# Expert blocks of two batches spread over two attention stages, and the sorting's counts copied out of their bank

## The chip, the cores and the metric

The kernel runs on one core of a Trainium2 chip. Its engines work side by side, each through its own queue in order: TensorE (PE, with weight loads PEld), VectorE (DVE), ScalarE (ACT), GpSimd (POOL) and SyncE (SP), which here issues most transfers. The metric is the time of one execution on the device in microseconds, the median over several runs; lower is better.

## What is computed

Four sequences of 1024 tokens with 128 features pass two layers. Each layer normalises, scales and shifts by a modulation of its batch's condition, and adds a gated result, first of a mixer and then of a mixture of experts. In the first layer the mixer is causal attention with 16 query heads, 4 key heads and rotary embedding; the experts are the best two of eight for every token.

```python
# layer 0
h = layernorm(x) * (1 + ca) + sa
x = x + ga * attention(h, Wq, Wk, Wv, Wo)
h = layernorm(x) * (1 + cb) + sb
scores = softmax(h @ gate_w.T)
topk_w, topk_idx = top_k(scores, 2);  topk_w /= sum(topk_w)
for e in range(8):
    g, u = split(h @ w1[e])
    out += combine[:, e] * (silu(g) * u @ w2[e])
x = x + gb * out
# layer 1: a selective scan in place of attention, then experts with a capacity
```

All arithmetic is in float32.

## The kernel before

**Attention** runs in eight stages, numbered 0 to 7 by `at`: for each of four batches b two head groups c (L686). A stage works eight tiles of 128 queries in the order 7, 0, 6, 1, 5, 2, 4, 3 (L685). A tile has four steps g. In each, `probabilities` (L586) multiplies queries by keys, masks and takes the smallest with VectorE, exponentiates with ScalarE and scales by the reciprocal sum on GpSimd (L618). One tile later `second_half` (L649) transposes the probabilities (L627), multiplies them by the values into the bank `po`, copies this to `aT` (L643) and projects it into `pw`, which is added to x (L189 and L190). Other work is woven between as Python generators that advance a step at a time: the next stage's projection, zeroing of buffers in HBM, and the two below.

**The first layer's experts.** Once both head groups of a batch are done, `sort_tokens` (L325) runs in the next stage with c = 0 (stages 2, 4 and 6 for batches 0, 1 and 2; batch 3 is sorted in the scan part). It normalises the batch, takes router logits, chooses two experts per token and counts, with matmuls by a triangle and by ones, how many tokens of each expert come before each token (bank `pin`). From `pin[:, TB, :]`, the totals, `find_blocks` works out which blocks of 128 slots belong to which expert; from `pin[:, :TB, :]` each token's slot follows. Sixteen indirect transfers then scatter the rows into HBM (L379). In the stage after it (3, 5 and 7) the class `Blocks` works the 23 blocks: `turn` transposes three blocks' rows, `first` multiplies one block by its expert's first weights and applies silu, `second` by the second weights and the gate. The weights come from HBM with three buffers (`fw`, L262), by transfers whose expert number SP reads from a register. `first` and `second` of a block share one PSUM bank. `first_returns` gathers the results back (L281) and adds them to x, by the program in the second head group's stage of the batch two later (stages 5 and 7).

**PSUM.** Pool `ps_m` has one bank, tag `m`. In attention the value projection, the features, the sorting's transposes, logits and counts, the blocks' `turn` and `first`/`second`, and `pw` take it by turns.

**Order.** The program's order gives priorities only. The tile framework places instructions on each engine's queue ahead of time: the earliest in the program that is ready by its own reckoning goes first, and a tile whose buffer is taken waits for its release. Work whose inputs are there early can thus run far ahead of its place in the program. On the chip each queue keeps the order so found.

**The loop before** steps the blocks so (L721 to L729), three blocks for every tile, and makes the object at the end of the preceding stage (L751 to L753):

```python
if blocks is not None:
    if g == 0:
        blocks.turn(n)
    else:
        blocks.second(3 * n + g - 1)
probabilities(i, g, q, k, pr)
if blocks is not None and g < 3:
    blocks.first(3 * n + g)
```

Of the kernel before, what the change touches and what calls it, by code (L numbers as in the profile page):

```python
# [11 lines left out]
F32 = mybir.dt.float32  # L12
# [6 lines left out]
P = 128  # L19
# [7 lines left out]
NE = 8  # L27
# [17 lines left out]
def mm(nc, out, lhsT, rhs, start=True, stop=True):  # L45
    return nc.tensor.matmul(out, lhsT, rhs, start=start, stop=stop)  # L46
# [3 lines left out]
def adaln_two_layers(ctx: ExitStack, tc: tile.TileContext, I: dict, out: bass.AP):  # L50
# [14 lines left out]
    def load(pool, name, eng=nc.sync):  # L65
# [6 lines left out]
    make_identity(nc, ident)  # L72
    ones = cst.tile([P, P], F32, name="ones")
    nc.gpsimd.memset(ones, 1.0)

    causal = cst.tile([P, P], F32, name="causal")
    nc.gpsimd.memset(causal, 0.0)
    nc.gpsimd.affine_select(
        out=causal, in_=causal, compare_op=ALU.is_ge, fill=NEG, base=0, pattern=[[-1, P]], channel_multiplier=1
    )  # L80

    before = cst.tile([P, P], F32, name="before")
    nc.gpsimd.affine_select(
# [44 lines left out]
    def drained(steps):  # L128

        while True:  # L130
            try:
                next(steps)
            except StopIteration as end:
                return end.value
# [174 lines left out]
    def find_blocks(total, nb, pool):  # L309


        over = pool.tile([P, NE, TB], F32, tag="f_over", bufs=1, name="f_over")
        nc.vector.tensor_tensor(over, total.unsqueeze(2).to_broadcast([P, NE, TB]), after, ALU.is_gt)
        blocks = pool.tile([P, NE], F32, tag="f_blocks", bufs=1, name="f_blocks")
        nc.vector.tensor_reduce(blocks, over, AX.X, ALU.add)
        upto = pool.tile([P, NE], F32, tag="f_upto", bufs=1, name="f_upto")
        nc.vector.tensor_tensor_scan(upto, ones[:, :NE], blocks, 0.0, ALU.mult, ALU.add)
        yield
        past = pool.tile([P, NB, NE], F32, tag="f_past", bufs=1, name="f_past")[:, :nb]
        nc.vector.tensor_tensor(past, number[:, :nb], upto.unsqueeze(1).to_broadcast([P, nb, NE]), ALU.is_ge)  # L320
        which = pool.tile([P, NB], F32, tag="f_which", bufs=1, name="f_which")[:, :nb]
        nc.vector.tensor_reduce(which, past, AX.X, ALU.add)
        return blocks, upto, which

    def sort_tokens(b, kept, pool, ps, tag, xtag="fxn"):  # L325


        xn = pool.tile([P, TB, D], F32, tag=xtag, bufs=1, name="fxn")
        yield from norm_steps(b * TB, TB, xn)
        hT = pool.tile([P, S], F32, tag=tag, bufs=1, name="fhT")  # L330
        yield from feature_steps(xn, hT, ps, modT[0][:, 4, b : b + 1], modT[0][:, 3, b : b + 1])
        pl = ps.tile([P, TB, NE], F32, tag="m", name="fpl")
        for t in range(TB):
            mm(nc, pl[:, t, :], hT[:, t * P : (t + 1) * P], f_gate)
        yield
        m1, m2, oh1, oh2 = yield from top2_steps(pl, sm)

        both = sm.tile([P, TB, NE], F32, tag="f_both", bufs=1, name="f_both")
        nc.vector.tensor_add(both, oh1, oh2)
        flat = both.rearrange("p t e -> p (t e)")  # L340
        pin = ps.tile([P, TB + 1, NE], F32, tag="m", name="fpin")
        pinf = pin.rearrange("p t e -> p (t e)")
        mm(nc, pinf[:, : TB * NE], before, flat, stop=False)
        for n in range(1, TB):
            mm(nc, pinf[:, n * NE : TB * NE], ones, flat[:, : (TB - n) * NE], start=False, stop=(n == TB - 1))
        mine = sm.tile([P, NE], F32, tag="f_mine", bufs=1, name="f_mine")
        nc.vector.tensor_reduce(mine, both.rearrange("p t e -> p e t"), AX.X, ALU.add)
        mm(nc, pin[:, TB, :], ones, mine)
        yield
        z = sm.tile([P, TB], F32, tag="f_z", bufs=1, name="f_z")  # L350
        nc.vector.scalar_tensor_tensor(z, m1, 1e-20, m2, ALU.add, ALU.add)
        nc.vector.reciprocal(z, z)
        w = keep.tile([P, 2, TB], F32, tag=f"f_w{b}", name="f_w")
        nc.vector.tensor_mul(w[:, 0], m1, z)
        nc.vector.tensor_mul(w[:, 1], m2, z)
        yield

        blocks, upto, which = yield from find_blocks(pin[:, TB, :], NB, sm)
        expert = keep.tile([P, NB], I32, tag=f"f_expert{b}", name="f_expert")
        nc.vector.tensor_scalar(expert, which, float(NE - 1), None, ALU.min)  # L360
        yield

        nc.vector.tensor_tensor(upto, upto, blocks, ALU.subtract)
        pos = sm.tile([P, TB, NE], F32, tag="f_pos", bufs=1, name="f_pos")
        nc.vector.scalar_tensor_tensor(
            pos, upto.unsqueeze(1).to_broadcast([P, TB, NE]), float(P), pin[:, :TB, :], ALU.mult, ALU.add
        )
        yield
        place = sm.tile([P, 2, TB], F32, tag="f_place", bufs=1, name="f_place")
        placei = keep.tile([P, 2, TB], I32, tag=f"f_placei{b}", name="f_placei")  # L370
        for k, oh in enumerate((oh1, oh2)):
            nc.vector.tensor_mul(oh, oh, pos)
            nc.vector.tensor_reduce(place[:, k], oh, AX.X, ALU.add)
            yield
        nc.vector.tensor_copy(placei, place)
        kept[b] = expert, placei, w
        for t in range(TB):
            for k in range(2):
                nc.gpsimd.indirect_dma_start(  # L379
                    out=f_in[b][:, :],  # L380
                    out_offset=bass.IndirectOffsetOnAxis(ap=placei[:, k, t : t + 1], axis=0),
                    in_=xn[:, t, :],
                    in_offset=None,
                )
                yield
# [71 lines left out]
    with ExitStack() as es:  # L457
# [21 lines left out]


        MW = 512 + QG
        mask = aw.tile([P, MW], F32, name="mask")
        nc.gpsimd.memset(mask, 0.0)
        for j in range(4):
# [200 lines left out]
        order = [7, 0, 6, 1, 5, 2, 4, 3]  # L685
        stages = [(b, c) for b in range(B) for c in range(2)]  # L686
        waiting = Steps(None, 0)
        blocks = None
        hT = features(0)
        made = []  # L690
        for _ in project(0, hT, made, at_once=True):
# [5 lines left out]
        for at, (b, c) in enumerate(stages):  # L697
            q, k = made
            if c == 0:
                v = values(hT)  # L700
            coming = Steps(None, 0)


            sorting = sort_tokens(b - 1, kept, ab, ps_m, "xn") if c == 0 and b > 0 else iter(())
            back = first_returns(b - 2, ab, 3) if c == 1 and b > 1 else iter(())
            early = first_features() if (b, c) == stages[-1] else iter(())
            for n, i in enumerate(order):
                if n == 5 and at + 1 < len(stages):

                    if c == 1:  # L710
                        hT = features(b + 1)
                    made = []
                    coming = Steps(project(stages[at + 1][1], hT, made), 5)
                long = i >= TB // 2
                keys = S if long else S // 2
                pr = [
                    ab.tile([P, 4, keys], F32, tag=f"pr{hp}{int(long)}", bufs=1, name=f"pr{hp}") for hp in range(2)
                ]
                for hp in range(2):
                    nc.gpsimd.memset(pr[hp][:, 0:3, i * P + QG : (i + 1) * P], 0.0)  # L720
                for g in range(4):  # L721
                    if blocks is not None:
                        if g == 0:
                            blocks.turn(n)
                        else:
                            blocks.second(3 * n + g - 1)
                    probabilities(i, g, q, k, pr)
                    if blocks is not None and g < 3:
                        blocks.first(3 * n + g)  # L729
                    waiting.take(-(-waiting.n // (4 - g)))  # L730
                    if n > 5 and g % 2 == 1 or n == 7 and g == 0:
                        coming.take(1)

                    if at < 2:
                        next(zeros, None)
                    if at == 0 and n == 0:
                        next(gates, None)

                    if n > 1:
                        next(sorting, None)  # L740
                        next(sorting, None)
                next(back, None)
                next(early, None)
                next(early, None)
                waiting = Steps(second_half(b, c, i, pr, v), i + 2)
            if at == 1:
                drained(zeros)
            drained(sorting)
            drained(back)
            drained(early)  # L750
            blocks = None  # L751
            if c == 0 and b > 0:
                blocks = Blocks(b - 1, ab, (ps_m, "m"), [(ps_m, "m")], rest)  # L753
        waiting.take(TB + 1)


# [718 lines left out]
```

## Time and profile before

| | us |
|---|---|
| median of 3 runs | 2087.29 |
| lowest and highest | 2079.24 and 2093.18 |
| the profiled execution | 2099.86 |
| its span, first to last instruction | 2098.1 |
| attention, to its last `aT` copy | 1390.7 |

The profile page gives each engine's busy time, then the span in 40 slices of 52.5 us with the busy share in tenths and the clock that was granted to TensorE. Below that stands what the groups of instructions cost and waited for. The two groups of GpSimd that matter here, with count, busy time and mean length, then idle time and its releaser:

```profile
L618 POOL TENSOR_SCALAR pr<-pr,den 128x32 f32<-128x32 f32 (+31 forms) x512 | 357.5, 714 | 311.0 <-DVE den L615 304.9
L379 POOL DMA_INDIRECT blocks_in<-fxn,f_placei x64 | 65.3, 1020 | 56.8 <-DMA blocks_in<-fxn,f_placei 46.5
```

### The profile page before, as it was taken

How to read it: one execution, taken by the hardware profiler on the slowest of the kernel's cores; microseconds unless marked ns; L12 is line 12 of the kernel's file. 1: busy time of each engine (PE TensorE's matmuls, PEld its weight loads, DVE VectorE, ACT ScalarE, POOL GpSimd, SP SyncE). 2: the span in 40 equal slices, each digit the busy share in tenths (PEclk: the TensorE clock that was granted, in tenths of full speed). 3: DMA queues.
4: the chain of work that ended last, by engine and by line, in shares of the span. 5: the costliest groups of instructions: out<-in, count | busy, mean ns of one | idle time of the engine just before them, and what ended most of it. 6: DMA issues, size and time to landing. Idle time of an engine off the chain costs nothing. (4 is left out here: it accounts for less than half of the span.)

```text
span 2098.1 us, 29043 instructions
## 1 busy us (share of the span) xinstructions
PE 1777.6 (85%) x8957; PEld 962.3 (46%) x8957; DVE 1325.2 (63%) x4000; ACT 948.5 (45%) x2073; POOL 1000.2 (48%) x1277
## 2 busy tenths in 40 slices
PE   5999899898999898999988899967769757748984
PEld 2444454453555344455534455533335423216764
DVE  6655666665667665666766466646768886972243
ACT  2353544743554554454365345544456345332221
POOL 3345434446333636532544643344663775672254
PEclk9899999999999998999999999988889977968996
DMA  7302001002222101222200122210012220003334
GB/s 232 133 1 51 1 5 47 1 29 73 60 70 75 41 1 46 79 63 70 77 13 24 43 75 67 61 40 3 29 48 86 79 103 17 4 25 95 115 127 149
DMA packets 103755, 123.58 MB, mean 59 GB/s; under 512 B 15024, under 2 KB 68656, under 8 KB 103600
## 3 DMA queue, kind: packets, MB, share of 16 engines
q1 hardware_dynamic: 83296, 97.70, 15.7%
q0 software_dynamic: 8192, 16.74, 2.6%
q10 hardware_dynamic: 12112, 7.29, 1.2%
q8 instruction: 71, 1.16, 0.2%
q14 instruction: 84, 0.69, 0.1%
HBM read 67.85 MB, written 32.90 MB: 48 GB/s over the span
## 5 line engine op out<-in xcount | busy, mean ns | idle before, releaser
L618 POOL TENSOR_SCALAR pr<-pr,den 128x32 f32<-128x32 f32 (+31 forms) x512 | 357.5, 714 | 311.0 <-DVE den L615 304.9
L612 ACT ACTIVATE pr<-pr,nb 128x32 f32<-128x32 f32 (+31 forms) x512 | 371.9, 728 | 156.1 <-DVE nb L599 147.7
L627 PE MATMUL pt<-ident,pr 128*128 128x128 f32 x2304 | 343.9, 284 | 52.4 <-POOL pr L618 43.2
L627 PEld LDWEIGHTS pt<-ident,pr 128*128 128x128 f32 x2304 | 255.0, 142 | 247.3 <-POOL pr L618 81.4
L46 PE MATMUL sc<-k,q 64*128 64x512 f32 (+14 forms) x1536 | 332.4, 524 | 31.5 <-DVE nb L599 24.3
L46 PE MATMUL po<-pT,v 128*64 128x512 f32 x1152 | 345.5, 626 | 2.6 <-DVE pT L631 2.6
L629 ACT COPY pT<-pt 128x512 f32<-128x512 f32 x288 | 167.7, 582 | 359.8 <-PE pt L627 306.0
L599 DVE CUSTOM_DVE_ANT_0 pr<-sc,mask 128x512 f32<-128x512 f32 (+15 forms) x512 | 273.0, 559 | 69.7 <-PE sc L46 58.4
L631 DVE COPY pT<-pt 128x512 f32<-128x512 f32 x288 | 198.3, 689 | 163.8 <-PE pt L627 147.4
L957 POOL TENSOR_TENSOR hc<-h,cc 128x512 f32<-128x512 f32 x128 | 162.0, 1279 | 101.0 <-DVE h L953 43.3
L46 PEld LDWEIGHTS sc<-k,q 64*128 64x128 f32 x1536 | 123.3, 192 | 183.3 <-DVE nb L599 87.3
L46 PE MATMUL pu<-du,spread 128*128 128x512 f32 x256 | 145.8, 672 | 52.2 <-DVE h L953 42.5
L720 POOL MEMSET pr<- 128x288 f32 x128 | 42.4, 340 | 258.4 <-PE pt L627 254.3
L599 DVE CUSTOM_DVE_ANT_0 pr<-sc,mask,nb 128x416 f32<-128x416 f32 (+15 forms) x256 | 120.0, 496 | 8.0 <-PE sc L46 6.9
L951 ACT ACTIVATE da<-dt,negA 128x512 f32<-128x512 f32 x128 | 91.6, 719 | 64.9 <-DVE h L953 64.4
L46 PEld LDWEIGHTS po<-pT,v 128*64 128x64 f32 x1152 | 69.5, 136 | 84.2 <-issue 42.9
L1343 POOL DMA_INDIRECT y<-slots_out,slot x56 | 56.7, 1013 | 94.0 <-PE ph L46 51.0
L949 DVE TENSOR_TENSOR pu<-pu,bb 128x512 f32<-128x512 f32 x128 | 85.1, 684 | 26.1 <-PE pu L46 15.7
L46 PEld LDWEIGHTS pu<-du,spread 128*128 128x128 f32 x256 | 44.9, 204 | 121.0 <-DVE h L953 73.7
L612 ACT ACTIVATION_READ_ACCUMULATOR pr<-pr,nb 128x1 f32 x512 | 96.5, 188 | 0.0
L568 POOL TENSOR_TENSOR q<-rot_u,rot_v 128x512 f32<-128x512 f32 x64 | 81.4, 1272 | 31.3 <-DMA rot_v<-rot_w 23.6
L379 POOL DMA_INDIRECT blocks_in<-fxn,f_placei x64 | 65.3, 1020 | 56.8 <-DMA blocks_in<-fxn,f_placei 46.5
(273 smaller groups left out, 2685.1 us busy)
## 6 DMA issues: line engine op xcount, KB each, us to landing
fw<-in_f_w SPq DMA_DIRECT2D x92, 320.0 KB
rot_v<-rot_w SPq DMA_DIRECT2D x300, 64.0 KB
gw<-in_g_w SPq DMA_DIRECT2D x15, 512.0 KB
fxe<-blocks_in SPq DMA_DIRECT2D x28, 192.0 KB
blocks_out<-fye SPq DMA_DIRECT2D x28, 192.0 KB
blocks_in<-mask SPq DMA_DIRECT2D x20, 256.0 KB
slots_in<-mask SPq DMA_DIRECT2D x16, 256.0 KB
g_w<-in_g_w SPq DMA_DIRECT2D x8, 512.0 KB
```

What stands on the lines that cost most here:

```text
L46: return nc.tensor.matmul(out, lhsT, rhs, start=start, stop=stop)
L379: nc.gpsimd.indirect_dma_start(out=f_in[b][:, :], out_offset=bass.IndirectOffsetOnAxis(ap=placei[:, k, t : t + 1], axis=0), in_=xn[:, t, : ...
L568: nc.gpsimd.tensor_add(to, u.rearrange("p (n q) -> p n q", q=QG), v.rearrange("p (n q) -> p n q", q=QG))
L599: nc.vector.tensor_tensor_reduce(out=pr[hp][:, g, lo:hi], in0=sc[:, hp, : hi - lo], in1=mask[:, MW - hi + lo :] if hi == nk else mask[:, : ...
L612: nc.scalar.activation(p, p, AF.Exp, bias=nb[:, last, hp : hp + 1], scale=-1.0, accum_out=den[:, hp : hp + 1])
L618: nc.gpsimd.tensor_scalar(p, p, den[:, hp : hp + 1], 1.0, ALU.mult, ALU.mult)
L627: next_to(hp == 0 and g == 0, lambda: nc.tensor.transpose(to, p, ident))
L629: nc.scalar.copy(pT[:, hp, :], pt)
L631: nc.vector.tensor_copy(pT[:, hp, :], pt)
L949: nc.vector.tensor_mul(pu, pu, bb[:, tok])
L951: nc.scalar.activation(da, dt[:, tok], AF.Exp, scale=negA[:, c : c + 1])
L957: nc.gpsimd.tensor_mul(hcs[-1], h, cc[:, tok])
```

## The change

Three things. First, the blocks of batches 0 and 1 are stepped over two stages each (3 and 4, 5 and 6) in place of one; batch 2 keeps stage 7 alone. A generator does the same steps in the same order and is advanced twice for every g; for batches 0 and 1 each step takes two advances, so that one step falls to each g, ahead of `probabilities`. A group of three blocks now takes two tiles of queries. The object, with its first weight loads, is made when the generator is first advanced. At the ends of stages 4, 6 and 7 what is left of it is run. Stages 4 and 6 thus hold sorting and blocks at once. Second, `sort_tokens` copies the whole count bank to a tile `ahead` in SBUF right after the counting, and later steps read the copy. Third, the causal mask's first form lives in a buffer of the tag `fam`, which the blocks use later, in place of one of its own, and is made after the first loads.

```diff
+        ahead = sm.tile([P, TB + 1, NE], F32, tag="f_ahead", bufs=1, name="f_ahead")
+        nc.vector.tensor_copy(ahead, pin)
...
-        blocks, upto, which = yield from find_blocks(pin[:, TB, :], NB, sm)
+        blocks, upto, which = yield from find_blocks(ahead[:, TB, :], NB, sm)
...
-            pos, upto.unsqueeze(1).to_broadcast([P, TB, NE]), float(P), pin[:, :TB, :], ALU.mult, ALU.add
+            pos, upto.unsqueeze(1).to_broadcast([P, TB, NE]), float(P), ahead[:, :TB, :], ALU.mult, ALU.add
...
-    causal = cst.tile([P, P], F32, name="causal")
+        causal = ab.tile([P, P], F32, tag="fam", name="causal")
...
-        blocks = None
+        def block_steps(b, fast):
+            blocks = Blocks(b, ab, (ps_m, "m"), [(ps_m, "m")], rest)
+            for j in range(0, NB, 3):
+                doing = [(blocks.turn, j // 3)]
+                for r in range(j, j + 3):
+                    doing += [(blocks.first, r), (blocks.second, r)]
+                for what, which in doing:
+                    what(which)
+                    yield
+                    if not fast:
+                        yield
+                yield
+                if not fast:
+                    yield
+
+        blocks = iter(())
...
-                    if blocks is not None:
-                        if g == 0:
-                            blocks.turn(n)
-                        else:
-                            blocks.second(3 * n + g - 1)
+                    next(blocks, None)
                     probabilities(i, g, q, k, pr)
-                    if blocks is not None and g < 3:
-                        blocks.first(3 * n + g)
+                    next(blocks, None)
...
-            blocks = None
+            if at + 1 == len(stages) or at == 4 or at == 6:
+                drained(blocks)
             if c == 0 and b > 0:
-                blocks = Blocks(b - 1, ab, (ps_m, "m"), [(ps_m, "m")], rest)
+                blocks = block_steps(b - 1, b == B - 1)
```

More of the change, by code (lines that the diff above doesn't have):

```diff
@@ L74, in adaln_two_layers @@
     nc.gpsimd.memset(ones, 1.0)
-    causal = cst.tile([P, P], F32, name="causal")
[L77 to L80, printed above, removed]
     before = cst.tile([P, P], F32, name="before")
@@ L481, in adaln_two_layers @@
         MW = 512 + QG
+        causal = ab.tile([P, P], F32, tag="fam", name="causal")
+        nc.gpsimd.memset(causal, 0.0)
+        nc.gpsimd.affine_select(
+            out=causal, in_=causal, compare_op=ALU.is_ge, fill=NEG, base=0, pattern=[[-1, P]], channel_multiplier=1
+        )
         mask = aw.tile([P, MW], F32, name="mask")
```

## The prediction

> **What bounds the kernel now.** I read the page first, for the engine that is nearly always busy.
>
> ```profile
> span 2098.1 us, 29043 instructions
> ...
> PE 1777.6 (85%) x8957; PEld 962.3 (46%) x8957; DVE 1325.2 (63%) x4000; ACT 948.5 (45%) x2073; POOL 1000.2 (48%) x1277
> ...
> PE   5999899898999898999988899967769757748984
> PEclk9899999999999998999999999988889977968996
> ```
>
> PE is the busy engine. The edits lie in attention, which ends near slice 27 of 40. So I cut attention into its eight stages 0 to 7, (batch, head group) in the program's order. Each stage works eight query tiles and ends here where its eighth copy aT<-po starts: 207.0, 356.4, 525.7, 700.8, 874.1, 1050.4, 1225.2 and 1390.7 us. The view of busy time by stretch for stages 1 to 7 (stretch, length, PE, PEld, DVE, ACT, POOL, granted clock, DMA share, GB/s):
>
> ```profile
> 207.00:356.40 149.40, 137.71 (x718) 67.17 (x718) 90.99 (x296) 73.10 (x174) 65.34 (x98) 0.99 0.08 19
> 356.40:525.70 169.30, 151.40 (x779) 76.68 (x780) 102.24 (x372) 86.36 (x201) 81.93 (x114) 0.95 0.12 32
> 525.70:700.80 175.10, 167.36 (x958) 95.12 (x958) 120.60 (x390) 84.98 (x203) 71.63 (x104) 1.00 0.25 70
> 700.80:874.10 173.30, 154.90 (x779) 77.56 (x780) 106.99 (x382) 86.21 (x201) 91.31 (x125) 0.93 0.13 35
> 874.10:1050.40 176.30, 168.88 (x958) 96.44 (x958) 120.77 (x390) 85.11 (x203) 71.77 (x104) 0.99 0.24 69
> 1050.40:1225.20 174.80, 152.56 (x779) 77.25 (x781) 106.79 (x375) 89.05 (x209) 91.08 (x125) 0.94 0.13 34
> 1225.20:1390.70 165.50, 156.84 (x936) 91.02 (x936) 105.20 (x362) 86.08 (x203) 51.64 (x84) 1.00 0.19 55
> ```
>
> Stages 2, 4, 6 sort a batch; 3, 5, 7 run its 23 blocks; stage 1 has neither. I split each length into PE work at full clock and loss. The loss is the idle time plus what the clock took, (1 - clock) x length. Stage 4: idle 173.3 - 154.9 = 18.4, clock 0.07 x 173.3 = 12.1, loss 30.5, work 142.8. So work/loss are 136.2/13.2 (stage 1), 142.9/26.4 (2), 167.4/7.7 (3), 142.8/30.5 (4), 167.1/9.2 (5), 142.1/32.7 (6), 156.8/8.7 (7). The three sorting stages agree on the work within 0.8 us, which supports the split. Block stages are PE work almost end to end; sorting stages lose about 30 us.
>
> Where do they lose it? The same view for shorter stretches: the first query tile of stages 2, 3, 4 and 6, then the seventh of stages 3 and 4.
>
> ```profile
> 356.40:397.70 41.30, 36.21 (x175) 16.86 (x176) 25.35 (x109) 28.24 (x66) 12.10 (x19) 0.96 0.00 1
> 525.70:564.50 38.80, 35.46 (x211) 20.00 (x211) 25.96 (x89) 19.57 (x47) 12.16 (x19) 1.00 0.22 65
> 700.80:746.40 45.60, 39.25 (x175) 17.43 (x176) 29.60 (x119) 28.20 (x65) 21.58 (x30) 0.89 0.05 14
> 1050.40:1095.20 44.80, 36.48 (x175) 16.54 (x176) 30.20 (x120) 28.06 (x65) 21.53 (x30) 0.96 0.05 14
> 658.10:685.90 27.80, 27.80 (x136) 14.54 (x136) 21.30 (x61) 12.28 (x31) 14.50 (x19) 1.00 0.31 78
> 828.70:862.60 33.90, 26.62 (x103) 11.71 (x104) 16.82 (x44) 10.57 (x26) 23.05 (x28) 0.90 0.26 67
> ```
>
> POOL carries 21.5 us in the first tile of stages 4 and 6 against 12.1 in stage 2: the 16 gathers of the preceding batch's results (689.1 to 715.6), which the scheduler has run almost a stage ahead of their place in the program. They cost 45.6 - 41.3 = 4.3 and 44.8 - 41.3 = 3.5 us, 3.9 on average. In the seventh tile PE idles 7.3 us and the clock takes 0.10 x 33.9 = 3.4. The timeline names the wait (start, length, engine, line, operation; in brackets the idle time and its releaser):
>
> ```profile
> 830.03 0.98 POOL L379 DMA_INDIRECT blocks_in<-fxn,f_placei  x1 [0.91 <-DMA blocks_in<-fxn,f_placei]
> 832.54 0.97 POOL L379 DMA_INDIRECT blocks_in<-fxn,f_placei  x1 [1.53 <-DMA blocks_in<-fxn,f_placei]
> 833.53 1.27 POOL L563 TENSOR_TENSOR k<-rot_u,rot_v 128x512 f32<-128x512 f32 x1
> 834.77 1.52 POOL L618 TENSOR_SCALAR pr<-pr,den 128x608 f32<-128x608 f32 x2
> 835.60 0.48 PE L627 MATMUL pt<-ident,pr 128*128 128x128 f32 x1 [6.16 <-POOL pr L618]
> ```
>
> Two scatters stand ahead of a softmax scaling on POOL; each waits for the one before to land; PE's next instruction in order is a transpose of that scaling's result.
>
> **The change, part by part.** *Half the blocks leave stages 3 and 5.* A stage's block work on PE is 167.4 - 136.2 = 31.2, half of it 15.6. For the loss at half the blocks I take the middle between stage 1 and the full stage. Stage 3: 167.4 - 15.6 + (13.2 + 7.7)/2 = 162.3, or -12.8. Stage 5: 167.1 - 15.6 + (13.2 + 9.2)/2 = 162.7, or -13.6.
>
> *They arrive in stages 4 and 6*: +15.6 of work each, against losses of 30.5 and 32.7. What fills? (a) The short waits: a full load of blocks cut stage 1's loss by 5.5, half of it gives 2.7. (b) The clock that the counting costs (below), 3.4 at most; I take half, 1.7. (c) The seventh tile's 7.3 + 3.4 = 10.7: its share of the block work is 15.6/8 = 2 us, and a filled stall also keeps some clock; I take 4.0. Together 8.4, so each pays 15.6 - 8.4 = +7.2. Bounds: with nothing filled +15.6; with the loss down to a block stage's 9 after the gathers have left, stage 4 is 142.8 + 15.6 + 9 = 167.4 (-5.9) and stage 6 142.1 + 15.6 + 9 = 166.7 (-8.1).
>
> *The gathers move.* They need the last blocks_out, which now comes late in stages 4 and 6, so they land at the start of 5 and 7: -3.9 twice and +3.9 twice, net 0. Stage 7's and 5's blocks could cover some of it, at most all 7.8; the scatters' tail just before them on POOL could add as much.
>
> The clock at the counting: the trace shows PE idle for only 1.5 us, and then fully busy at about half clock for 8 us, behind matmuls only 8 to 64 columns wide.
>
> ```profile
> 784.00:788.00 4.00, 2.50 (x16) 1.15 (x12) 4.00 (x20) 1.84 (x4) 1.16 (x4) 1.00 0.00 0
> 788.00:792.00 4.00, 4.00 (x21) 2.67 (x20) 2.77 (x14) 0.00 (x0) 1.61 (x2) 0.56 0.00 0
> 792.00:796.00 4.00, 4.00 (x16) 1.64 (x13) 2.31 (x11) 2.37 (x5) 0.15 (x1) 0.59 0.22 63
> ```
>
> That is (0.44 + 0.41) x 4 = 3.4 us, the bound of (b); 128-column block matmuls amid them may keep the clock. [...]
>
> *Small edits.* `ahead` adds a 72-column VectorE copy per batch. The nearest rows read 64 columns of the same bank in 211 and 225 ns, so about 0.9 us over four batches. Three lie beside attention, where scatters end (846.9) 20 us before the next blocks' first turn (866.7); the fourth adds 0.2 in the scan part. The earlier release frees the bank by about 3 us (readings at 440.6 and 443.7). I take 0, between -3 and +1. The causal mask's two POOL instructions (0.20 and 0.28 us) move behind the first loads, where POOL idles until 25.2: 0. Blocks are made when first stepped, with the first three weight loads on SP. For batch 1 they now wait for batch 0's buffers instead of running at 794; with rot_v queued behind them on SP, a late one would hold the next projection. The three loads took under 5 us (794.0 to 798.8), and the last buffer frees four head steps, some 20 us, before the next block: 0, at worst +5 a pair. Weight loads now run beside the scatters. Near 1140 three did: the scatters stood 3.4 to 4.9 us apart, otherwise 2.5 to 3, and that tile of stage 6 took 26.2 against 20.4. I take 0, since that burst goes too; at worst +6 in stage 4.
>
> Sum: -12.8 + (7.2 - 3.9) + (-13.6 + 3.9) + (7.2 - 3.9) + 3.9 = -12.0 of the profiled 2099.9 (span 2098.1 and 1.8 around it), which lies 0.6% above the median, 2087.3. On the median: **2075**.
>
> **The rivals.** *The one PSUM bank becomes the bound (slower).* Tag m has one buffer. A block holds it from its first matmul to the gated copy: 519.2 to 525.0, 5.8 us. In stages 4 and 6 it must also serve the eight value tiles, four sorting tiles and eight output projections. For: four sorting waits of 5.8 are 23 us, over the roughly 18 between the last scatter's landing and the next turn; beyond that PE stops at the turn, in order. An output projection that waits keeps aT, and so the next po. Against: stage 3 lives with 23 such holds, and the counts leave the bank sooner. Price: nothing filled (8.4 each) and half a hold, 2.9, in the four short tiles of both stages: -12.0 + 16.8 + 23.2 = +28, or 2115.
>
> *All of it fills (faster).* Both sorting stages end with a loss of 9: -12.8 - 5.9 - 13.6 - 8.1 + 7.8 = -32.6, or 2055. For: block stages do hold 7.7 and 9.2. Against: the scatters' waits are POOL's, and PE stays in order.
>
> *The blocks do not spread.* The scheduler runs ready work early, as with the gathers, so stages 3 and 5 could stay full: about 2087. Against: block steps in the trace keep the program's spacing, some 7 us.
>
> **How the numbers follow.** About 1%, 21 us, is what a measurement of this kernel can tell from no change. Forecast 0.40, own range 2059 to 2092: (b) and (c) whole give 8.4 more in each stage, -12.0 - 16.8 = -28.8; (a) to (c) at nothing give -12.0 + 16.8 = +4.8. Of it 0.13 lies beyond -21. All fills 0.25, nearly all beyond. No spreading 0.10. The bank 0.25, of which 0.03 stays within 1%. So faster 0.37, within 0.41, slower 0.22. The range reaches over most of the fill and half of the bank's case: 2050 to 2108.
>
> **What would show it.** Stages 3 and 5 near 162 and 166, 4 and 6 near 177 and 178; gathers at the starts of 5 and 7; a clock above 0.95 in stages 4 and 6; the sorting's last scatter still ahead of the next turn. Wrong if PE in stage 4 waits at pf, pw or tp for the bank, or if stages 4 and 6 grow by 15 or more.

## The result, and the profile after

The changed kernel takes 2116.89 us (median of 4 runs, 2110.98 to 2123.33) against 2088.42 us for the kernel before (4 runs, 2079.24 to 2093.18): 1.0154 times as long, with a 95% interval of 1.0125 to 1.0182. That is 28.5 us slower. The forecast was 2075, and the result lies above its range.

The page of the changed kernel, the same lines as before:

```profile
span 2115.3 us, 29053 instructions
...
PE 1800.4 (85%) x8957; PEld 974.4 (46%) x8957; DVE 1326.5 (63%) x4004; ACT 951.4 (45%) x2077; POOL 999.6 (47%) x1277
...
PE   6999899898999998799999889968779757757994
PEclk9899999999999999899999999988878867877998
```

TensorE's share of busy time is 85% in both, with 22.8 us more of it and not one matmul more. The span alone grew by 17.2 us, less than the timed difference. The last part, behind the last copy of the experts' results in the second layer (`ye`), takes 62 to 64 us in eleven of the 16 profiled executions and 74 in five, with either layout of the code. The execution of before that was profiled took 73.9 there, the changed one 63.0. So below, kernels are compared by the ratio to runs of the kernel before beside them, and profiles by stage.

The view of busy time by stretch for stages 3 to 7 of the changed kernel, cut as before at each stage's eighth copy of `aT` (stretch, length, PE, PEld, DVE, ACT, POOL, granted clock, DMA share, GB/s):

```profile
524.10:687.80 163.70, 155.74 (x837) 82.17 (x837) 104.33 (x340) 78.52 (x188) 65.43 (x98) 1.00 0.17 49
687.80:883.80 196.00, 172.80 (x906) 93.88 (x908) 123.76 (x435) 92.25 (x217) 97.77 (x130) 0.94 0.19 54
883.80:1047.10 163.30, 154.89 (x831) 81.47 (x831) 103.89 (x339) 78.12 (x186) 65.46 (x98) 1.00 0.17 48
1047.10:1238.30 191.20, 171.60 (x905) 93.60 (x906) 121.74 (x429) 95.38 (x226) 97.71 (x130) 0.95 0.19 55
1238.30:1402.90 164.60, 156.06 (x930) 90.20 (x930) 104.06 (x359) 85.58 (x203) 51.43 (x84) 1.00 0.18 54
```

The matmuls did move (958 to 837 in stage 3, 779 to 906 in stage 4). Stages 3 and 5 became 11.4 and 13.0 us shorter, stages 4 and 6 became 22.7 and 16.4 longer. Split as in the prediction, the losses of stages 3 to 6 sum to 80.1 us before and 80.5 after: in sum nothing was filled. The work at full clock grew from 619.4 to 633.6 us. Profiles of other kernels below, with nearly the same order of TensorE's instructions in attention, repeat this: four like the old kernel have work of 618.4 to 622.8 us and losses of 72.8 to 81.5, two like the changed one work of 634.9 and 636.2 and losses of 76.7 and 77.1. (Stage 4: idle 196.0 - 172.8 = 23.2, clock 0.06 x 196.0 = 11.8, loss 35.0, work 161.0.)

Stage 4 in four stretches, the first tile, tiles two to six, the seventh and the eighth:

```profile
687.80:729.00 41.20, 39.69 (x208) 21.22 (x209) 29.20 (x121) 29.22 (x69) 12.10 (x19) 0.96 0.12 35
729.00:825.80 96.80, 88.04 (x519) 51.98 (x520) 62.05 (x237) 47.77 (x114) 44.92 (x66) 0.96 0.15 45
825.80:862.20 36.40, 27.66 (x101) 11.00 (x101) 21.28 (x54) 9.37 (x22) 28.63 (x32) 0.91 0.33 90
862.20:883.80 21.60, 17.41 (x81) 9.67 (x83) 11.22 (x25) 5.88 (x12) 12.12 (x15) 0.84 0.24 66
```

Before, these took 45.6, 82.3, 33.9 and 11.5 us:

```profile
746.40:828.70 82.30, 77.53 (x433) 41.45 (x434) 53.83 (x207) 43.47 (x104) 40.40 (x60) 0.96 0.09 26
862.60:874.10 11.50, 11.50 (x74) 6.96 (x73) 6.73 (x14) 3.97 (x9) 6.28 (x8) 1.00 0.32 84
```

(The first tile and the seventh stand in the prediction.) The first tile lost the gathers (POOL 21.6 to 12.1 us) and 4.4 us. The middle took the blocks in, +14.5. The last two tiles, where the stall was to be filled, grew by 2.5 and 10.1. The timeline of their end says why (start, length, engine, line, operation; in brackets the idle time and its releaser):

```profile
866.71 0.95 POOL L275 DMA_INDIRECT fy<-blocks_out,f_placei  x1 [0.30 <-DVE den L617]
867.97 0.95 POOL L275 DMA_INDIRECT fy<-blocks_out,f_placei  x1 [0.30 <-DVE rot_u L531]
868.96 0.70 POOL L620 TENSOR_SCALAR pr<-pr,den 128x512 f32<-128x512 f32 x1
869.72 1.11 PE L629 MATMUL pt<-ident,pr 128*128 128x128 f32 x4 [3.09 <-POOL pr L620]
```

L275 is a gather of the preceding batch's results, L620 the softmax scaling, L629 the transposes that wait for it. The gathers run from 834 to 868, close behind the last scatter (829.7) and between the scalings, and TensorE waits for the scaling behind them. The old kernel had them at the end of stage 3 and in the first tile of stage 4, and they have moved to the place where POOL was already late.

### The profile page after: what moved, and what is told of

Its sections match the earlier page's. It is cut to its first block, busy times and chain, and to the rows that moved or that the text cites. A ratio compares the mean times of both kernels' runs of the same rounds, so it can differ in the third digit from the quotient of the medians.

```text
span 2115.3 us, 29053 instructions
## 1 busy us (share of the span) xinstructions
PE 1800.4 (85%) x8957; PEld 974.4 (46%) x8957; DVE 1326.5 (63%) x4004; ACT 951.4 (45%) x2077; POOL 999.6 (47%) x1277
## 4 chain that ended last, share of the span: by engine, by line
PE 52%; DVE 17%; POOL 10%; ACT 8%; issue 7%; DMA 6%; SPq 0%; ACTq 0%; POOLq 0%; DVEq 0%
PE po L46 13%; PE pt L629 11%; PE sc L46 5%; ACT pr L614 5%; PE pf L46 4%; DVE h L969 4%; POOL pr L620 4%; DVE pr L601 3%; PE ph L46 3%; PE ypy L46 3%; PE proj L46 3%; PE pw L46 2%; PE pu L46 2%; POOL hc L973 2%; DMA blocks_in<-fxn,f_placei 2%
## 5 line engine op out<-in xcount | busy, mean ns | idle before, releaser
L620 POOL TENSOR_SCALAR pr<-pr,den 128x32 f32<-128x32 f32 (+31 forms) x512 | 356.2, 710 | 306.3 <-DVE den L617 300.8
L629 PE MATMUL pt<-ident,pr 128*128 128x128 f32 x2304 | 350.9, 287 | 51.9 <-POOL pr L620 40.3
L629 PEld LDWEIGHTS pt<-ident,pr 128*128 128x128 f32 x2304 | 259.2, 144 | 248.5 <-POOL pr L620 81.0
L46 PE MATMUL po<-pT,v 128*64 128x512 f32 x1152 | 356.5, 629 | 4.5 <-DVE pT L633 4.4
L46 PE MATMUL sc<-k,q 64*128 64x512 f32 (+14 forms) x1536 | 327.2, 516 | 28.5 <-DVE nb L601 23.1
L631 ACT COPY pT<-pt 128x512 f32<-128x512 f32 x288 | 167.4, 581 | 383.3 <-PE pt L629 324.6
L973 POOL TENSOR_TENSOR hc<-h,cc 128x512 f32<-128x512 f32 x128 | 162.7, 1283 | 128.9 <-DVE h L969 51.6
L46 PE MATMUL pu<-du,spread 128*128 128x512 f32 x256 | 153.6, 712 | 39.4 <-DVE h L969 33.0
L46 PEld LDWEIGHTS pu<-du,spread 128*128 128x128 f32 x256 | 49.8, 221 | 109.1 <-DVE h L969 54.8
L46 PEld LDWEIGHTS pf<-fxT,fw 128*128 128x128 f32 x552 | 75.8, 205 | 49.0 <-ACT fxT L407 14.9
```

The source lines that it names most:

```text
L620: nc.gpsimd.tensor_scalar(p, p, den[:, hp : hp + 1], 1.0, ALU.mult, ALU.mult)
L629: next_to(hp == 0 and g == 0, lambda: nc.tensor.transpose(to, p, ident))
L631: nc.scalar.copy(pT[:, hp, :], pt)
L973: nc.gpsimd.tensor_mul(hcs[-1], h, cc[:, tok])
```

## The experiments

A measured figure is the ratio to the kernel before, with its 95% interval. Expectations in us suppose about 2087 for the kernel before; where it took another time, they are read by ratio. "Attention's end" is the last `aT` copy in the profile, 1390.7 before and 1402.9 after.

### The halves of the loss

**The small edits alone**: the kernel before with the copy and the mask's move, the blocks stepped as of old.

```diff
+        ahead = sm.tile([P, TB + 1, NE], F32, tag="f_ahead", bufs=1, name="f_ahead")
+        nc.vector.tensor_copy(ahead, pin)
...
+        causal = ab.tile([P, P], F32, tag="fam", name="causal")
```

> The kernel before with the count copy and the moved causal mask, without the spreading. Theory POOL tail (the gathers now run on POOL right behind the scatters, in the projection's part of stages 4 and 6) and theory full price (the block work that arrives in stages 4 and 6 is simply paid, nothing there can be filled) both say no change: 2082 to 2094 us against 2088, scan part after attention at 707 us as before. Theory side edits (the 5 us that the scan part grew by, 707.4 to 712.4, come from the copy) says scan part 712 and 2093 or more.

Measured: 1.0052 (1.0031 to 1.0073). What I had priced at nothing is a third of the loss. Attention ends at 1383.1, no later than before. The time lies in the scan part: from the end of batch 1's scan to the end of batch 3's it takes 204.1 us, against 193.0 before and 205.4 in the changed kernel.

**The change without the last batch's copy, and that copy alone.** The first leaves the copy out for batch 3, whose sorting runs in the scan part. The second is the kernel before, with the mask moved and the copy for batch 3 only.

```diff
-        ahead = sm.tile([P, TB + 1, NE], F32, tag="f_ahead", bufs=1, name="f_ahead")
-        nc.vector.tensor_copy(ahead, pin)
+        ahead = pin
+        if b < B - 1:
+            ahead = sm.tile([P, TB + 1, NE], F32, tag="f_ahead", bufs=1, name="f_ahead")
+            nc.vector.tensor_copy(ahead, pin)
```

> The changed kernel with the count copy made for batches 0 to 2 only; batch 3, sorted in the scan part, reads its bank as before. The order that the framework lays out on TensorE is then that of the changed kernel in attention and that of the kernel before after it. Theory scan order (the copy for the last batch makes the framework lay the scan part out anew, with four more loads of ScalarE's tables, and that costs 10 to 14 us): the part after attention falls from 712 to about 698, total 2101 to 2106. If the scan part's growth is noise or comes from being started later: total 2115 to 2119.

> The kernel before, mask moved, with the count copy for batch 3 only: attention in the order of before, the scan part in the order of the changed kernel. Scan order: 2096 to 2100, all of it after attention. Rival: 2087.

Measured: 1.0074 (1.0047 to 1.0102) and 1.0072 (1.0048 to 1.0096). The kernel before took 2100.66 us beside them. By ratio the first lies within what was expected (2101 to 2106 of 2087), the second a little above (2096 to 2100). The two sum to 1.5%, the whole loss. Behind attention, without the last part, the first takes 641.8 us and the second 649.1; the kernel before took 633.5 and the changed one 649.4. Laid beside each other, the first kernel has TensorE's order of the changed kernel in attention and that of before behind it; the second has it the other way round. All 16 profiles fit this: the five with TensorE's scan order of the changed kernel take 203.8 to 205.7 us from the end of batch 1's scan to the end of batch 3's, the ten with that of before 188.4 to 195.9 (a third order comes below). In the scan part the order of the second pulls ScalarE's functions apart. The groups of table loads, before and then with the last copy alone (line, engine, operation, count, busy time, mean ns, idle before):

```profile
L951 ACT ACT_TABLE_LOAD x8 | 10.3, 1283 | 1.0 <-DVE h L953 0.9
L902 ACT ACT_TABLE_LOAD x4 | 5.1, 1283 | 0.1
```

```profile
L955 ACT ACT_TABLE_LOAD x12 | 15.4, 1283 | 3.6 <-DVE h L957 3.4
L906 ACT ACT_TABLE_LOAD x6 | 7.7, 1283 | 0.1
```

L951 and L955 are one source line, the scan's exponential; L902 and L906 the silu of its gate. Other lines have two fewer, so there are 62 loads in place of 58.

**The spreading with no copy at all.**

```diff
-        ahead = sm.tile([P, TB + 1, NE], F32, tag="f_ahead", bufs=1, name="f_ahead")
-        nc.vector.tensor_copy(ahead, pin)
...
-        blocks, upto, which = yield from find_blocks(ahead[:, TB, :], NB, sm)
+        blocks, upto, which = yield from find_blocks(pin[:, TB, :], NB, sm)
```

> The changed kernel without the count copy: block spreading and moved mask alone. Scan part in the order of before. If the early release of the bank does nothing in attention: as with the copy for three batches, within 4 us. If the bank bounds stages 4 and 6: these two grow by 5 or more each, the sorting's first scatter comes later than 95 us into the stage.

Measured: 1.0081 (1.0053 to 1.0110), as with three copies. The first scatters come 93.4 and 92.8 us into stages 4 and 6. For batches 0 to 2 the copy neither helps nor harms, as far as these runs can tell.

**Is it the copy, the bank's early release, or that one order?** Two more kernels from the last-copy one: in the first the copy is made but not read, so the bank is freed no earlier; in the second ScalarE makes it.

```diff
-            ahead = sm.tile([P, TB + 1, NE], F32, tag="f_ahead", bufs=1, name="f_ahead")
-            nc.vector.tensor_copy(ahead, pin)
+            spare = sm.tile([P, TB + 1, NE], F32, tag="f_ahead", bufs=1, name="f_ahead")
+            nc.vector.tensor_copy(spare, pin)
```

```diff
-            nc.vector.tensor_copy(ahead, pin)
+            nc.scalar.copy(ahead, pin)
```

> The kernel before with the mask moved; for batch 3 alone the count bank is copied, but the later steps go on reading the bank, so that it isn't freed earlier. The order of instructions after attention is then that of before, with one VectorE copy more. Theory 'the bank freed early lets the scan part be laid out anew, and that order is slower': ratio 1.000, between 0.998 and 1.002, 58 table loads on ScalarE, third and fourth segment of the scan part together 193 us. Rival 'the copy itself stands in the way, behind the counting': 1.005 to 1.007, as with the copy in use.

> As the run with the copy for batch 3 alone, in use, but ScalarE makes the copy. The bank is freed as early, and the scan part is laid out in a third order, neither that of before nor that of the changed kernel. Theory 'an early release of the bank is what costs, in whatever order': 1.007, the third and fourth segment 204 us. Theory 'it is that one order, with its four more table loads and da pieces pulled apart': 58 or 59 table loads and 0.998 to 1.003. Neither if it is above 1.01 or below 0.995: then orders scatter, and no cause can be named from two of them.

Measured: 0.9999 (0.9983 to 1.0016) and 1.0039 (1.0025 to 1.0053). The copy itself costs nothing; with it unread there are 58 loads, the old order in the scan part, and 193.2 us in the two segments. The third order has 58 loads too, 195.5 us there, and the part behind attention takes 704.7 us against 698.3. So the earlier release, that is, the later steps' reading of the copy in place of the bank, is what lets the framework lay the scan part out anew, and both orders that came of it are slower, by 0.4% and 0.5 to 0.7%. The second expectation fell between its two theories. The four extra loads are 4 x 1.28 = 5.1 us of ScalarE of some 15; which instructions make up the rest isn't shown.

### The gathers

**Gathers held back**, in the changed kernel and in the one before: each may not be issued ahead of the zeroing of `pr` of the tile that the program gives it, in stages 5 and 7.

```diff
+                with tc.issue_after(behind[-1].ins) if behind else nullcontext():
+                    nc.gpsimd.indirect_dma_start(
...
-                    nc.gpsimd.memset(pr[hp][:, 0:3, i * P + QG : (i + 1) * P], 0.0)
+                    behind.append(nc.gpsimd.memset(pr[hp][:, 0:3, i * P + QG : (i + 1) * P], 0.0))
```

> The changed kernel with each pair of gathers of batches 0 and 1 queued on POOL behind the probability-buffer memset of the tile in which the program asks for them, so two gathers a tile over stages 5 and 7. POOL tail: stages 4 and 6 fall from 196.0 and 191.2 to about 184 and 180, stages 5 and 7 grow by 1 to 3 each; total 2117 - 20 = about 2097. Full price: stages 4 and 6 stay above 192 and 187; total 2108 or more.

> The kernel before with its gathers held in the same way. Both theories: the first tiles of stages 4 and 6 lose the 4.3 and 3.5 us that they had over stage 2, stages 5 and 7 get 1 to 2 each: 2080 to 2086 against 2088. If a gather costs nothing wherever it stands: 2088.

Measured: 1.0143 (1.0109 to 1.0177) and 1.0049 (1.0032 to 1.0065). In the changed kernel stages 4 and 6 gave back 14.3 and 3.1 us, and stages 5 and 7 took 7.2 and 9.5. In the old kernel stages 4 and 6 fell by 4.0 and 5.3, and 5 and 7 rose by 9.9 and 10.7. Summed that is -0.7 and +11.3: the stages pay for the gathers wherever they stand, and in the old kernel they pay more in stages 5 and 7. Neither expectation for the old kernel had this.

**Gathers left out**, in both kernels, and with them the adding of these two batches' expert results.

```diff
-            back = first_returns(b - 2, ab, 3) if c == 1 and b > 1 else iter(())
+            back = iter(())
```

> The changed kernel without the gathers of batches 0 and 1 and without adding them: the first layer's expert results of these two batches are left out. POOL tail: stages 4 and 6 near 183 and 179, total 2090 to 2096, a little under the held version. Full price: stages 4 and 6 above 190 and 186, total 2105 or more.

> The kernel before without the gathers of batches 0 and 1 and without adding them (their first layer's expert results are left out), as the counterpart of the changed kernel without them (2096). POOL tail: gathers cost 8 here and about 20 in the changed kernel, so 2079 to 2082, stages 4 and 6 at 169 to 171. Full price: gathers cost the same in both, so this takes as much less than 2087 as the changed kernel did, 2066 to 2070.

Measured: 1.0033 (1.0015 to 1.0051) for the changed kernel without them, and 0.9909 (0.9881 to 0.9937) for the old one. They cost 1.2% of the changed kernel and 0.9% of the old, so a worse place of the gathers explains about 0.3%, which the intervals don't tell from nothing, and 1.25% remains between the two kernels without them. My theory at that point, that scatters and gathers in one line on POOL were the loss, fell with this pair. Stage 4 without gathers, in the old and then the changed kernel:

```profile
698.60:864.60 166.00, 150.42 (x779) 76.03 (x781) 102.33 (x372) 86.04 (x201) 81.66 (x114) 0.96 0.12 33
```

```profile
687.90:868.30 180.40, 166.19 (x906) 90.76 (x908) 117.03 (x419) 92.12 (x218) 81.89 (x114) 0.98 0.18 52
```

The stage's idle and clock losses fell (22.2 to 17.8), as the forecast had it for the whole change. The seventh tile went from 34.4 to 27.6 us, the eighth from 11.5 to 15.8. In stage 6 the loss did not fall (23.3 to 25.2). And the work of stage 4 at full clock is 18.8 us more, while stage 3 was relieved of 10.0 (165.3 to 155.3).

### What the work is made of

The two traces were then compared matmul by matmul. I gave each one the time from its start to the next one's start, or to its own end if that came first, and summed by the tile written, in us (not corrected for the clock):

| tile | stage 3 before | after | stage 4 before | after | stages 3 to 6, before | after |
|---|---|---|---|---|---|---|
| `pf`, `ftp` (blocks) | 33.5 | 17.5 | 1.8 | 21.6 | 71.7 | 76.9 |
| `po` (attention) | 40.5 | 42.9 | 40.1 | 42.5 | 160.8 | 170.7 |
| `pt` (attention) | 37.1 | 38.3 | 38.9 | 40.4 | 152.9 | 159.1 |
| `sc` (attention) | 37.1 | 37.5 | 43.2 | 39.8 | 159.4 | 153.9 |

The blocks' own matmuls divide roughly evenly: 16.0 us left stage 3, and 19.8 came to stage 4, at its lower clock. What doesn't stand still is attention's own: the same 144 matmuls of `po` in a stage take 2.4 to 2.6 us longer in all four stages of the changed kernel. The same can be read from the view of busy time of `po` alone, stages 3 and 4, before and then after (stretch, length, PE, clock, DMA share, GB/s):

```profile
525.70:700.80 175.10, 42.96 (x144) 1.00 0.25 70
700.80:874.10 173.30, 42.30 (x144) 0.93 0.13 35
```

```profile
524.10:687.80 163.70, 45.45 (x144) 1.00 0.17 49
687.80:883.80 196.00, 44.86 (x144) 0.94 0.19 54
```

The clock hides part of this. With each matmul's time multiplied by the clock granted while it ran, all matmuls of the four stages go from 623.4 to 634.9 us: `po` from 159.3 to 166.2, `pt` from 151.0 to 153.5, the blocks from 70.9 to 72.0, `sc` from 150.8 to 151.0. So the blocks' work did divide, and what grew is `po` and `pt` above all.

For `po` in stages 3 and 5 the traces show how. Its matmuls come in pairs, one for each half of a head group with 64 columns of weights, and a pair that starts together runs side by side: in stage 3 of the old kernel two start at 547.392 and 547.398 and take 643 ns each. In the first tile of stage 3 of the changed kernel the second of a pair starts 0.25 to 0.48 us late six times in a row, each time within 0.06 us of the end of VectorE's copy of its half of `pT` (copy to 549.44, starts 549.02 and 549.49). In the stages at or near full clock, `po` goes by the number of matmuls that start within 60 ns of the one before:

| | starts together | `po`, us |
|---|---|---|
| stages 3 and 5, before, gathers left out | 62 | 38.6 |
| stage 7, both kernels | 61 | 38.4 |
| stages 3 and 5, before | 57 | 40.5 |
| stages 3 and 5, changed | 52 | 42.9 |

In stages 4 and 6 there are 62 and 60 such starts before and 61 in each after, and corrected for the clock `po` grew by 1.2 and 0.7 us. That, and what `pt` gained, isn't explained by it.

**Blocks at the old density in every second tile.** If single steps with little to overlap were the reason, three blocks in one tile and none in the next should restore the old work.

```diff
-                    if not fast:
-                        yield
                 yield
-                if not fast:
+                for _ in range(0 if fast else 8):
                     yield
```

> As the changed kernel with the count copy for batches 0 to 2, but a group of three blocks is stepped in one tile, at the density of the kernel before, and the next tile has none; so half the blocks a stage, in the old pattern. Theory single steps (a block step that stands alone on TensorE costs more than one beside another; TensorE's time in stages 3 to 6 rose by 13 us with the same instructions): stages 3 and 5 fall from 164.0 and 163.4 to about 160, stages 4 and 6 from 194 and 191 to about 188 and 186; within 3 us of the kernel before in all. Theory any half (the first half of the blocks costs more than the second however they are stepped): stages as in the changed kernel, 0.6 to 0.9% slower than before.

Measured: 1.0098 (1.0072 to 1.0125), with the copy of batch 3 left out; the change without that copy had 1.0074. Its stages 3 and 4:

```profile
525.60:688.30 162.70, 154.93 (x837) 81.23 (x837) 104.23 (x340) 78.24 (x188) 65.64 (x99) 1.00 0.18 50
688.30:885.30 197.00, 174.01 (x906) 91.64 (x908) 122.94 (x434) 92.39 (x217) 97.73 (x130) 0.95 0.18 53
```

The work is 154.9 and 164.2 us, about as in the changed kernel (155.7 and 161.0) or worse. The theory of single steps fell: the density within a tile isn't it.

**Scatters of batches 1 and 2 left out**, in the changed kernel (without batch 3's copy) and in the one before; their blocks then work on zero rows.

```diff
-        for t in range(TB):
+        for t in range(0 if b in (1, 2) else TB):
```

> The changed kernel with the count copy for batches 0 to 2, without the scatters of batches 1 and 2, whose expert blocks then work on zero rows: their sorted inputs are left out. Stages 4 and 6 lost 33 and 28 us in idle time and clock with them. If the scatters' waits on POOL own what block work could not fill: stages 4 and 6 fall to about 176, loss 12 to 15, and the difference to the kernel before without scatters is the extra TensorE time alone, 13 us over the four stages. If the short waits of the in-order queue own it: stages 4 and 6 stay above 185.

> The kernel before without the same scatters, the counterpart. If the scatters own the loss: stages 4 and 6 at about 160 (work 143 and a loss as in stage 1, 13, and the gathers), total 2% below. If not: above 168.

Measured: 1.0027 (1.0011 to 1.0043) and 0.9899 (0.9874 to 0.9923). The old kernel gains 1.0%, its stages 4 and 6 falling to 163.3 and 162.4. The changed one gains some 0.5% against its copy-less form, and its stages 4 and 6 stay at 189.1 and 187.0, with losses of 27.0 and 25.7. So the scatters' waits aren't what the blocks failed to fill. Without scatters the last two tiles of stage 4 still take 33.8 and 22.1 us, against 25.2 and 11.8 in the old kernel without scatters; without gathers they took 27.6 and 15.8. It is the gathers, in their new place, that hold these tiles up; the stage as a whole is longer without them too (180.4 after 166.0).

**The old density, begun one tile later**, so that only the last blocks reach stages 4 and 6; also without batch 3's copy.

```diff
+            for _ in range(0 if fast else 8):
+                yield
+            blocks = Blocks(b, ab, (ps_m, "m"), [(ps_m, "m")], rest)
```

> The blocks of batches 0 and 1 at the density of the kernel before but begun one tile later, so that only the last group runs in the first tile of stages 4 and 6; count copy for batches 0 to 2. If block work in that first tile is filled into its 5 to 6 us of idle time: stages 3 and 5 fall by 3, stages 4 and 6 grow by 0 to 1; 4 us less than before. If it is paid in full, or the gathers, now a tile later, cost more there: same as before or up to 6 us slower.

Measured: 0.9997 (0.9979 to 1.0015). The generator's stepping costs nothing, and a small shift gains nothing. It also shows that `po` isn't a matter of the number of blocks alone: reckoned as in the table, its stage 3 has 42.1 us of `po` beside 21 blocks, where the old kernel has 40.5 beside 22 (the first of its 23 runs at the end of stage 2). It has 53 starts together, the old kernel 57. No kernel tried was faster than the kernel before, except those that leave work out.

## Why the prediction was wrong

**The step that failed first is the sum's +15.6 and -15.6 for half the blocks.** I took TensorE's busy time at full clock as a stock that divides: (167.4 - 136.2)/2. Stage 3 was relieved of 11.7 and stage 5 of 12.2 us, while 18.2 and 19.9 came to stages 4 and 6. Stage 1 before and stage 3 of both kernels show it: no blocks 136.2, half of them 155.7, all 167.4, so the first half costs 19.5 us and the second 11.7. Against the forecast that is 14.2 us over the four stages. It isn't the blocks that resist division: corrected for the clock they take 1.1 us more (7 of their matmuls came to stage 6 from stage 7), `po` 6.9 and `pt` 2.5. Of `po` 4.8 us are in stages 3 and 5, where fewer pairs start together. Why the rest grew stays open.

**The second is "filled 8.4".** With the gathers' 3.9 us each, the losses of stages 4 and 6 were to fall to 18.2 and 20.4 us and were 35.0 and 29.2. (b) held in its place: at the counting the clock took 1.7 us, as forecast, in place of 3.4.

```profile
768.00:772.00 4.00, 3.29 (x25) 2.32 (x23) 2.89 (x17) 2.50 (x6) 0.94 (x2) 1.00 0.00 0
772.00:776.00 4.00, 4.00 (x23) 3.42 (x24) 2.73 (x12) 1.88 (x4) 1.11 (x3) 0.63 0.00 0
776.00:780.00 4.00, 4.00 (x20) 1.42 (x18) 2.77 (x14) 0.70 (x3) 1.93 (x3) 0.94 0.26 70
```

But the stage's whole clock loss is 11.8, after 12.1: the eighth tile, at full clock before, now loses 0.16 x 21.6 = 3.5. (c) failed: the seventh tile's loss went from 10.7 to 8.7 + 0.09 x 36.4 = 12.0, and the eighth idles 4.2. With the gathers left out the seventh tile did become shorter, so part of this failure is the gathers' new place. What was filled is the first tile, whose idle time went from 6.4 to 1.5.

**The gathers' move** was forecast to the starts of stages 5 and 7, net 0. They run at the ends of 4 and 6. A net of 0.3% (1.2 less 0.9) is small, as forecast, but not by the forecast way; and the price of 3.9 us for a set of 16 was wrong. Without them the old kernel gains 0.91% of 2100.66, 19 us for two sets: the first tile was not the only one that paid. Stages 3 and 5, where the first gathers of a set run, are 3.4 and 4.5 us shorter without them.

**The small edits** were priced at 0 between -3 and +1, and "the fourth adds 0.2 in the scan part". The copy is that cheap, but it frees a bank, and that changes the scan part's order: 0.5 to 0.7%, 11 to 15 us. This term alone, put right, would have made the forecast no change. The mask's move cost nothing, as forecast (0.9999 with it). A small misreading that carries nothing: the next blocks' first turn starts at 866.1, not 866.7.

**The rivals.** The bank as the bound gave 2115, close to the time by luck and not by its mechanism: the first scatters of stages 4 and 6 come 94.8 and 93.6 us into the stage, after 101.4 and 91.7 before, so the sorting isn't late; no wait of TensorE's matmuls at `pf`, `ftp`, `tp` or `pw` in these stages is over 0.7 us; and the copy that frees the bank in attention makes no difference. Its 16.8 for nothing filled came true, its 23.2 for the bank did not. That blocks do not spread is refuted by the counts. That the rest fills is refuted by the losses. Of the signs of being wrong the second came: stages 4 and 6 grew by 22.7 and 16.4.

The Trainium skill, "Perfetto Trace Analysis", section "Optimization Strategy", says that where the most-contended engine changes over time, interleaving those regimes may improve a kernel. Here TensorE was the busiest engine in both kinds of stage, and part of the loss to be filled was waiting for POOL: 80.1 us of loss before the interleaving, 80.5 after.

## What to carry over

A stage's busy time is no stock to be divided: the moved work may divide and the work beside it change, as `po` did here. Before work is spread, compare stretches with none, some and all of it, and price the first part by a stretch that has little. A stall that an in-order queue takes from another engine need not be filled by giving the queue more work of its own; look at what the moved work's successors will be queued behind. With a framework that lays out the order by itself, an edit that frees a buffer earlier can re-order code far from it, so compare the instruction orders first, and time small edits alone.

## Not expected of the hardware

- The 144 `po` matmuls of a stage took between 38.4 us of TensorE (stage 7 of both kernels) and 45.2 (stage 4 with the blocks in every second tile), reckoned as in the table, with the same shapes. Corrected for the clock the second is 40.9, and the most is 42.9 (stages 3 and 5 of the changed kernel, at full clock). Two that start together take hardly longer than one: four of one block of keys end 1.08 us after the first start (547.39 to 548.47, before), and 1.55 when the pairs come apart (549.02 to 550.57, changed).
- In the counting's stretch the clock fell to 0.63 within 4 us after a stretch (768 to 772) with 0.7 us of idle time.
- A table load on ScalarE takes 1.28 us. The Trainium skill, "ScalarE: Activation LUTs", section "What ACT_TABLE_LOAD costs", gives the same 1283 ns and adds a drain of 1380 ns; in the trace of the kernel with the last copy alone a load at 1501.00 is followed by its activation at 1502.29, and the instruction before it ended at 1500.98, so no drain shows. By the page an estimate for four loads is 10.6 us, by the trace it is 5.1.
